# Turning the quantized probabilities of the second layer by transposing DMAs

## The chip, the core and the metric

The kernel runs on one core of a Trainium2 chip. The core has a matrix engine (TensorE, PE in the profile, its weight loads PEld), a vector engine (VectorE, DVE), an activation engine (ScalarE, ACT), a general engine (GpSimd, POOL) and a queue engine (SyncE, SP) that issues DMAs. Matmuls and transposes on TensorE write to PSUM, from where VectorE or ScalarE has to copy the result to SBUF. DMAs move data between SBUF and device memory, or inside SBUF, on 16 DMA engines that all queues share. The metric is the device time of one execution in microseconds; less is better.

## The reference

Four transformer layers are applied in a row to `x` (16 sequences of 128 tokens, width 256, 16 heads of 16 features). The change concerns the second layer, whose two attentions work with numbers rounded to 8 bits:

```python
def _fq(x, delta, zp, n_bits):
    xi = _round_ste(x / delta) + zp
    xq = jnp.clip(xi, 0.0, 2.0 ** n_bits - 1.0)
    return (xq - zp) * delta

def _attn(x, ctx, wq, wk, wv, wo, bo, dq, dk, dv, dw):
    ...
    sim = jnp.einsum('bhid,bhjd->bhij', _fq(q, dq, 128.0, 8), _fq(k, dk, 128.0, 8)) * SCALE
    attn = jax.nn.softmax(sim, axis=-1)
    out = jnp.einsum('bhij,bhjd->bhid', _fq(attn, dw, 0.0, 8), _fq(v, dv, 128.0, 8))
    out = out.transpose(0, 2, 1, 3).reshape(b, n, D)
    return out @ wo + bo

h1 = _ln(x, ln1_g, ln1_b)
x = _attn(h1, h1, a1_wq, ...) + x
h2 = _ln(x, ln2_g, ln2_b)
x = _attn(h2, context, a2_wq, ...) + x
```

The probabilities `attn`, divided by the step `dw`, rounded and clipped, are whole numbers from 0 to 255, which bf16 holds exactly. The first, third and fourth layers use unrounded attentions and feed-forward blocks in float32.

## The kernel before

**Tiling.** The 16 sequences are split into 8 groups of two (`GB = 2`). `group(g)` (line 1330) writes down all steps of one group through the four layers; all eight groups can be under way together (`LIVE = 8`). Most working tiles are blocks cut out of one SBUF arena (kind `m`, called `arena` in the profile). PSUM has four slots of 2 KB per partition (`pw`) and a single one of 8 KB (`ps`) for attention scores.

**The stage of the change.** `quantized_attention` (line 1045) runs twice per group (`i = 0, 1`). It makes rounded queries, keys and values and calls `attention` (line 886), its only caller. For each of the two sequences `j`, `begin` computes the scores of all 16 heads into `ps`; then for each half `c` of eight heads `soft` (line 1097) makes the row maximum (line 1099), subtracts it (1112), takes the exponential (1118), sums and inverts (1124 to 1127), scales and rounds on GpSimd (eight instructions at line 1133) and clips into a bf16 block `eb` of 128 queries x 8 heads x 128 keys (DVE, line 1137). The product with the values needs the keys on the partitions, so `eb` has to be turned: eight 128x128 transposes on TensorE (line 905) into one `pw` slot, and one copy of 128x1024 bf16 to the block `eT`, on ScalarE (line 910) or VectorE (line 911). When both halves are there, `products` (line 867, sixteen matmuls at line 879) multiplies them with the values, and line 1143 scales the result. There are 8 groups x 2 attentions x 2 sequences x 2 halves = 64 such turns, and 32 products. The `dtype == F32` side of `attention` is not used here; the float32 attentions have a function of their own, whose products also appear at line 879.

**The order.** Nothing is scheduled on the chip: `Plan.order()` (line 217) writes the instruction order of every engine out in advance. Each step lists its possible engines with a price in us; the loop takes the step that can start earliest, ties being broken by its depth plus an entry of the table `LEADS` for its group and stage. A DMA step on SP is taken to be there at its price plus `LOAD = 2.2` plus an own extra after it starts (line 414). Blocks with a role are limited per stage by the counts given to `plan.enter` (line 889). On the chip every engine runs its list strictly in order, so an instruction that waits holds back all that stand behind it on that engine. All DMAs go through SP: weights (`weight`, line 629, 256 KB each, at most three in a stage), the first layer's rearrangements through device memory (lines 952, 974, 1029, 1036), and kept keys and values (lines 1192, 1216). SP too waits in order, for the data to store or for the place to load into.

Of the kernel before, what the change touches and what calls it, by code (L numbers as in the profile page):

```python
# [8 lines left out]
F32 = mybir.dt.float32  # L9
# [7 lines left out]
P = 128  # L17
B, S, D, H, DH, FF = 16, 128, 256, 16, 16, 1024
# [54 lines left out]


LEADS = [
    [83, 27, 167, 130, 306, 193, 74, 226, 213, -45, 163, -53, 159, -84, 116, -64, 214, 400, 286, 283],
    [-69, -856, -114, -260, -60, 57, -165, -14, -2, -22, -386, -90, 144, -71, -260, -59, -586, -159, -213, -106],
    [49, -47, -11, 314, -162, 407, 51, 168, -361, -27, -172, 141, -4, -107, 36, 5, -54, 235, 78, 92],
    [-16, -228, 250, -173, -19, 106, 36, 203, -176, 14, 164, 2, 299, -144, 10, 309, -45, 154, 150, -1],
    [210, 166, 422, 222, 201, 790, 324, 499, 569, 334, 435, 116, 502, 205, 259, 760, 536, 716, 652, 178],  # L80
    [330, 158, 210, 147, 392, 517, 262, 488, 490, 57, 292, 77, 380, 208, 348, 38, 542, 447, 523, 1141],
    [267, 148, 130, 158, 333, 376, 220, 605, 204, -29, 43, 216, 340, 164, 196, 435, 324, 999, 754, 951],
    [288, 156, 593, 320, 407, 313, 255, 389, 233, 323, -30, 86, 440, 164, 213, 583, 372, 760, 452, 550],
]
CONTEXT = 18
HANDOVER = {"PE": 0.25, "-": 0.0}
# [65 lines left out]
class Plan:  # L152
# [3 lines left out]
    def block(self, kind, shape, dtype=F32, role=None):  # L156
        b = Block(kind, shape, dtype)
        if role is not None:
            sec = self.section
            b.section, b.role, b.turn = sec, role, sec.made[role]  # L160
            sec.made[role] += 1
            sec.units[role] = max(sec.units[role], b.units)
        return b
# [264 lines left out]
def decoder_stack_kernel(ctx: ExitStack, tc: tile.TileContext, a: dict, out: bass.AP):  # L428
    nc = tc.nc
    V, A, G, T = nc.vector, nc.scalar, nc.gpsimd, nc.tensor  # L430
# [7 lines left out]
    ident = const.tile([P, P], F32, tag="ident", name="ident")  # L438
    make_identity(nc, ident)
    ident_b = const.tile([P, P], BF16, tag="identb", name="ident_b")  # L440
# [70 lines left out]
    plan = Plan()  # L511
    step, block = plan.step, plan.block
# [4 lines left out]
    def psum(dtype=F32, shape=(P, 2, NT)):  # L517
        return block("pw", shape, dtype)
# [110 lines left out]
    def weight(source):  # L629

        t = block("m", [P, 2, D], role="w")
        t.source = source.tensor.name, source.offset
        step(
            [("SP", 1.3, lambda: nc.sync.dma_start(out=t.ap(), in_=source.rearrange("(k p) m -> p k m", p=P)))],
            writes=[t],
        )
        return t
# [44 lines left out]
    def tokens_first(w, t, ps, lhs=None, start=True, stop=True, reads=(), holds=()):  # L682


        def issue():
            for j in range(GB):
                for k in range(2):
                    T.matmul(  # L688
                        ps.ap()[:, j, :], lhsT=lhs(k, j) if lhs else t.ap()[:, k, j * S : (j + 1) * S],
                        rhs=w.ap()[:, k, :], start=start and j + k == 0, stop=stop and j == GB - 1 and k == 1,  # L690
                    )

        step([("PE", 1.72, issue)], reads=[w, *([t] if t else []), *reads], writes=[ps], holds=holds)
# [192 lines left out]
    def attention(x, wo, begin, soft, out_of, vz, dtype, after):  # L886


        plan.enter(after=after, w=1, oT=1, e=2, eT=2, **({"r": 1} if dtype == F32 else {"eb": 1}))
        wo = weight(wo)  # L890
        oT = block("m", [P, 2, NT], role="oT")
        for j in range(GB):
            ps, held = begin(j)
            eTs = []
            for c in range(2):
                e = soft(ps, j, c, held[c])
                eT = block("m", [P, 8, S], dtype, role="eT")
                eTs.append(eT)
                per = 4 if dtype == F32 else 8
                for q0 in range(0, 8, per):  # L900
                    pt = block("pw", [P, per, S], dtype)

                    def turn(pt=pt, e=e, q0=q0):
                        for q in range(per):
                            T.transpose(pt.ap()[:, q, :], e.ap()[:, q0 + q, :], ident if dtype == F32 else ident_b)  # L905

                    step([("PE", 0.5, turn)], reads=[e], writes=[pt], holds=[eT])
                    step(
                        [
                            ("ACT", 0.6 if dtype == F32 else 1.2, lambda pt=pt, eT=eT, q0=q0: A.copy(eT.ap()[:, q0 : q0 + per, :], pt.ap())),  # L910
                            ("DVE", 0.66 if dtype == F32 else 0.7, lambda pt=pt, eT=eT, q0=q0: V.tensor_copy(eT.ap()[:, q0 : q0 + per, :], pt.ap())),
                        ],
                        reads=[pt], writes=[(eT, q0)],
                    )
            out_of(oT, eTs, vz, j)
        ps = psum()
        tokens_first(wo, oT, ps)
        add_to(x, ps)
# [551 lines left out]
```

## Time and profile before

| What | us |
|---|---|
| Time, median of 3 runs | 1461.99 (1459.98 to 1463.36) |
| The profiled execution | 1458.82 |
| Its span, first to last instruction | 1456.7 |
| TensorE busy | 1398.3 (96%) |
| VectorE busy | 1010.9 (69%) |
| ScalarE busy | 849.7 (58%) |
| GpSimd busy | 633.3 (43%) |
| DMA queue of SP, share of the 16 engines | 24.5% |

The groups of instructions in the profile are read as: line, engine and operation, output <- input with shape, count, then the busy time of the group and the mean duration of one. TensorE overlaps successive matmuls, so a group's count times its mean is more than the time that it holds the engine; the timeline of starts is the better measure.

### The profile page before, as it was taken

What the parts mean: (1) busy time and instruction counts of PE and PEld (TensorE: products, weight loads), DVE (VectorE), ACT (ScalarE), POOL (GpSimd) and SP (SyncE); (2) the same over time, 40 slices, a digit from 0 to 9 for tenths busy, and PEclk for the clock granted to TensorE, in tenths of its full rate; (3) what the DMA queues carried; (4) which work ended last, traced back from release to release, by engine and by line L of the source; (5) the groups of instructions that cost most, each with busy time, mean ns of one, the idle gap of its engine ahead of it and who ended that gap; (6) DMA issues with size and microseconds to landing.
All of it is one profiled execution on the core that took longest, in us unless ns stands there. A gap on an engine that the chain in (4) does not pass through costs nothing. (4 is left out here: it accounts for less than half of the span.)

```text
span 1456.7 us, 35756 instructions
## 1 busy us (share of the span) xinstructions
PE 1398.3 (96%) x14771; PEld 1141.3 (78%) x14771; DVE 1010.9 (69%) x1555; ACT 849.7 (58%) x1490; POOL 633.3 (43%) x1415
## 2 busy tenths in 40 slices
PE   8899998999899999899999999999999999999998
PEld 6677887878678888687878777777878888787777
DVE  1665788898988779767764976779478766556431
ACT  4565676766776656565554665657556454445552
POOL 2232857455777446524432542545634234243210
PEclk9999998999999999999999999999999999999999
DMA  6566513412432122112211532211210111100000
GB/s 207 138 171 192 188 48 102 117 34 67 125 90 95 44 67 70 56 52 66 84 38 45 160 101 97 85 55 56 73 45 2 42 38 66 31 31 2 2 9 23
DMA packets 138386, 109.67 MB, mean 75 GB/s; under 512 B 72288, under 2 KB 127472, under 8 KB 138096
## 3 DMA queue, kind: packets, MB, share of 16 engines
q1 hardware_dynamic: 138224, 107.40, 24.5%
q8 instruction: 116, 1.90, 0.5%
q14 instruction: 46, 0.38, 0.1%
HBM read 80.11 MB, written 27.26 MB: 74 GB/s over the span
## 5 line engine op out<-in xcount | busy, mean ns | idle before, releaser
L688 PE MATMUL pw<-arena 128*128 128x256 f32 x2048 | 484.2, 387 | 7.3 <-ACT arena L654 3.1
L675 PE MATMUL pw<-arena 128*128 128x256 f32 x2048 | 480.9, 385 | 7.8 <-ACT arena L663 2.5
L688 PEld LDWEIGHTS pw<-arena 128*128 128x128 f32 x2048 | 383.0, 192 | 68.8 <-issue 9.3
L675 PEld LDWEIGHTS pw<-arena 128*128 128x128 f32 x2048 | 379.2, 191 | 71.0 <-issue 10.0
L1133 POOL TENSOR_SCALAR arena<-arena,sm 128x128 f32<-128x128 f32 x512 | 195.9, 403 | 107.7 <-DVE sm L1127 73.4
L1314 DVE RECIPROCAL arena<-pw 128x256 f32<-128x256 f32 x64 | 112.1, 1752 | 104.0 <-PE pw L879 86.8
L734 POOL TENSOR_TENSOR arena<-arena,rows 128x512 f32<-128x512 f32 x107 | 137.7, 1289 | 89.7 <-ACT arena L721 74.0
L833 PE MATMUL ps<-arena 32*128 32x128 f32 (+2 forms) x3328 | 153.0, 309 | 2.8 <-DVE arena L1112 1.1
L1236 DVE TENSOR_REDUCE sm<-ps 128x16 f32<-128x2048 f32 x48 | 109.6, 2283 | 36.3 <-PE ps L833 33.8
L833 PEld LDWEIGHTS ps<-arena 32*128 32x128 f32 x3072 | 116.1, 186 | 20.4 <-issue 12.0
L696 DVE TENSOR_TENSOR arena<-pw,arena 128x512 f32<-128x512 f32 x88 | 60.3, 685 | 101.2 <-PE pw L688 99.7
L801 ACT ACTIVATE arena<-pw,cols_sb 128x256 f32<-128x256 f32 x184 | 78.0, 472 | 68.3 <-PE pw L675 65.5
L1261 POOL CAST mq<-sm 128x16 bf16<-128x16 f32 x58 | 15.8, 273 | 234.2 <-DVE sm L1236 114.6
L710 POOL TENSOR_SCALAR sm<-sm 128x2 f32<-128x2 f32 x88 | 20.6, 234 | 215.0 <-DVE sm L705 200.1
L721 ACT ACTIVATE arena<-arena,sm,sm 128x256 f32<-128x256 f32 x149 | 83.2, 597 | 49.3 <-POOL sm L714 48.7
L663 ACT ACTIVATE arena<-pw,cols_sb 128x256 f32<-128x256 f32 x140 | 72.7, 563 | 50.5 <-PE pw L647 47.0
L1275 ACT COPY arena<-pw 128x512 bf16<-128x512 bf16 x64 | 37.3, 582 | 84.5 <-PE pw L1271 77.6
L879 PE MATMUL pw<-arena 128*32 128x128 f32 (+1 forms) x2560 | 82.9, 265 | 3.4 <-ACT arena L910 3.0
L1099 DVE TENSOR_REDUCE sm<-ps 128x8 f32<-128x1024 f32 x64 | 77.6, 1213 | 9.8 <-PE ps L833 9.5
L1302 ACT ACTIVATE arena<-ps 128x1024 f32<-128x1024 f32 x64 | 64.1, 1025 | 33.1 <-PE ps L833 30.3
L647 PE MATMUL pw<-ident,arena 128*128 128x128 f32 x416 | 66.8, 286 | 15.1 <-DMA arena<-in_x_dram 5.1
L910 ACT COPY arena<-pw 128x1024 bf16<-128x1024 bf16 x56 | 56.3, 1011 | 41.9 <-PE pw L905 37.2
(142 smaller groups left out, 1993.8 us busy)
## 6 DMA issues: line engine op xcount, KB each, us to landing
arena<-in_L_xattn_ff_w_dram SPq DMA_DIRECT2D x38, 256.0 KB, 3.0
mha<-arena SPq DMA_DIRECT2D x16, 512.0 KB, 4.5
ca<-arena SPq DMA_DIRECT2D x16, 512.0 KB, 3.9
arena<-mha SPq DMA_DIRECT2D x16, 512.0 KB, 4.4
arena<-ca SPq DMA_DIRECT2D x16, 512.0 KB, 4.5
dqkv<-arena SPq DMA_DIRECT2D x8, 768.0 KB, 4.0
arena<-dqkv SPq DMA_DIRECT2D x16, 384.0 KB, 4.3
arena<-in_L_xattn_W_dram SPq DMA_DIRECT2D x24, 256.0 KB, 2.8
```

The source lines that it names most:

```text
L663: ("ACT", 0.54, lambda c=c: A.activation(dst.ap()[:, c, :], ps.ap()[:, c, :], AF.Identity, bias=biases(c), scale=scales(c))),
L675: T.matmul(ps.ap()[:, m, :], lhsT=w.ap()[:, k, m * P : (m + 1) * P], rhs=t.ap()[:, k, :], start=(k == 0), stop=(k == 1),)
L688: T.matmul(ps.ap()[:, j, :], lhsT=lhs(k, j) if lhs else t.ap()[:, k, j * S : (j + 1) * S], rhs=w.ap()[:, k, :], start=start and j + k == 0 ...
L721: ("ACT", 0.6, lambda j=j: A.activation(xh.ap()[:, j, :], x.ap()[:, j, :], AF.Identity, bias=nb.ap()[:, j : j + 1], scale=rstd.ap()[:, j : ...
L734: ("POOL", 1.33, lambda: G.tensor_tensor(dst.ap(), src.ap(), row(name), op)),
L801: "ACT", 0.47, lambda ps=ps, h=h, m=m, bias=bias: A.activation(h.ap()[:, m, :], ps.ap()[:, m, :], func, bias=bias),
L833: T.matmul(ps.ap()[:, s, c] if i is None else ps.ap()[:, s, c, i], lhsT=left(r, c) if i is None else left(r, c, i), rhs=right(r, c), start ...
L879: T.matmul(po.ap()[32 * s : 32 * s + 32, 2 * ones + c, :], lhsT=lhsT, rhs=eTs[c].ap()[:, 2 * s + i, :], start=(i == 0), stop=(i == 1),)
L1099: step([("DVE", 1.22, lambda: V.tensor_reduce(paired(m.ap()), ps.ap()[:, :, c], AX.X, ALU.max, negate=True))], reads=[ps], writes=[m])
L1133: G.tensor_scalar(e.ap()[:, q, :], e.ap()[:, q, :], r.ap()[:, q : q + 1], MAGIC, ALU.mult, ALU.add)
L1236: V.tensor_reduce(m.ap(), ps.ap().rearrange("p s c i k -> p (s c i) k"), AX.X, ALU.max, negate=True)
L1314: step([("DVE", 1.75, lambda po=po, r=r: V.reciprocal(r.ap(), po.ap()[:, 2:4, :]))], reads=[po], writes=[r])
```

## The change

The eight transposes and the copy of each turn are replaced by one DMA issued by SP that transposes in flight, from `eb` in SBUF to `eT` in SBUF (256 KB, bf16). Its price in the plan is 1.2 with an extra of 1.0, so that the plan takes its result to be there 1.2 + 2.2 + 1.0 = 4.4 us after it starts. The stage may hold two `eb` blocks in place of one, and the table `LEADS` has other numbers, so the instruction order of every engine differs throughout the kernel. The turn no longer uses a `pw` slot.

```diff
 LEADS = [
-    [83, 27, 167, 130, 306, 193, 74, 226, 213, -45, 163, -53, 159, -84, 116, -64, 214, 400, 286, 283],
...
+    [17, -123, 275, 177, 313, 413, 69, 330, 469, -222, 295, 20, 190, -607, -60, 168, 130, 288, 268, -9],
...
 ]
...
     def attention(x, wo, begin, soft, out_of, vz, dtype, after):
-        plan.enter(after=after, w=1, oT=1, e=2, eT=2, **({"r": 1} if dtype == F32 else {"eb": 1}))
+        plan.enter(after=after, w=1, oT=1, e=2, eT=2, **({"r": 1} if dtype == F32 else {"eb": 2}))
...
                 e = soft(ps, j, c, held[c])
                 eT = block("m", [P, 8, S], dtype, role="eT")
                 eTs.append(eT)
-                per = 4 if dtype == F32 else 8
-                for q0 in range(0, 8, per):
-                    pt = block("pw", [P, per, S], dtype)
-
-                    def turn(pt=pt, e=e, q0=q0):
-                        for q in range(per):
-                            T.transpose(pt.ap()[:, q, :], e.ap()[:, q0 + q, :], ident if dtype == F32 else ident_b)
-
-                    step([("PE", 0.5, turn)], reads=[e], writes=[pt], holds=[eT])
-                    step(
-                        [
-                            ("ACT", 0.6 if dtype == F32 else 1.2, lambda pt=pt, eT=eT, q0=q0: A.copy(eT.ap()[:, q0 : q0 + per, :], pt.ap())),
-                            ("DVE", 0.66 if dtype == F32 else 0.7, lambda pt=pt, eT=eT, q0=q0: V.tensor_copy(eT.ap()[:, q0 : q0 + per, :], pt.ap())),
-                        ],
-                        reads=[pt], writes=[(eT, q0)],
-                    )
+                step(
+                    [("SP", 1.2, lambda e=e, eT=eT: nc.sync.dma_start_transpose(out=eT.ap(), in_=e.ap().rearrange("p q k -> p (q k)")), None, 1.0)],
+                    reads=[e], writes=[eT],
+                )
             out_of(oT, eTs, vz, j)
```

## The prediction

> **What bounds the kernel now.** I read the page's busy shares first, then its chain of waits, then the group of the removed instructions, and last the DMA issues that resemble the added one.
>
> ```profile
> PE 1398.3 (96%) x14771; PEld 1141.3 (78%) x14771; DVE 1010.9 (69%) x1555; ACT 849.7 (58%) x1490; POOL 633.3 (43%) x1415
> ...
> PE 29%; DVE 1%; ACT 0%; issue 0%; ACTq 0%
> ```
>
> TensorE is busy for 1398.3 of 1456.7 us, so it idles for only 58.4. The chain that ended last, which the profile follows back over the last 30% of the span, is matmul after matmul. So TensorE's own list of work is the bound, and time taken off it is worth close to its length as long as nothing makes TensorE wait instead. Time taken off ScalarE (58% busy) is worth nothing by itself.
>
> The next fence is the groups by line; the two lines after the dots are the answer for line 905 by stages of the span (us, then TensorE and weight-load busy time of that line alone).
>
> ```profile
> L905 PE MATMUL pw<-ident_b,arena 128*128 128x128 bf16 x512 | 40.2, 222 | 5.2 <-DVE arena L1137 2.6 <-DVE arena L1315 1.1 <-ACT arena L1058 0.9
> L905 PEld LDWEIGHTS <-arena 128*128 128x128 bf16 x512 | 32.2, 99 | 16.3 <-DVE arena L1137 7.0 <-issue 5.0 <-DVE arena L696 0.3
> L910 ACT COPY arena<-pw 128x1024 bf16<-128x1024 bf16 x56 | 56.3, 1011 | 41.9 <-PE pw L905 37.2 <-issue 3.5 <-ACT arena L1058 0.7
> ...
> 150.00:400.00 250.00, 14.99 (x184) 12.08 (x184) 0.97 0.32 96
> ...
> sum 1457.00, PE 40.17 PEld 32.22; mean PE 6.69 PEld 5.37
> ```
>
> The 512 transposes have a busy time of 40.2 us, but that counts the overlap with their neighbours. The timeline of TensorE shows what they really hold it for:
>
> ```profile
> 817.00 1.89 PE L688 MATMUL pw<-arena 128*128 128x256 f32 x8
> 818.73 0.61 PE L905 MATMUL pw<-ident_b,arena 128*128 128x128 bf16 x8
> 819.17 3.67 PE L675 MATMUL pw<-arena 128*128 128x256 f32 x16
> 822.68 0.61 PE L905 MATMUL pw<-ident_b,arena 128*128 128x128 bf16 x8
> 823.13 1.95 PE L688 MATMUL pw<-arena 128*128 128x256 f32 x8
> ```
>
> The start of the transposes lies 0.44 and 0.45 us ahead of the start of the next matmul. Added up over all rows of line 905 in the timeline, with the idle time shown in the next row taken out, it is 33.2 us, or 0.52 per turn.
>
> The added operation does not occur in this trace: no DMA transposes. The nearest are DMAs cut into short pieces, in the answers for lines 974 and 1029 (issue time in ns as min/median/max) and in the list of DMA issues (KB each, median us from issue to landing):
>
> ```profile
> L974 SPq DMA_DIRECT2D arena<-dqkv x16: 359/377/1157, 25.4 to 832.0; - x16
> ...
> DMA to landing us min/median/max: 3.6/4.3/6.3
> ```
>
> ```profile
> L1029 SPq DMA_DIRECT2D do<-arena x64: 313/486/1837, 47.9 to 857.3; - x64
> ```
>
> ```profile
> do<-arena SPq DMA_DIRECT2D x64, 32.0 KB, 2.3
> ...
> arena<-in_L_xattn_W_dram SPq DMA_DIRECT2D x24, 256.0 KB, 2.8
> ```
>
> **The change part by part.** The sum is made against the profiled execution: 1458.82 us, of which 1456.7 are span and 2.1 lie around it. The median of the runs is 3.2 us above it.
>
> *Removed from TensorE:* 64 turns of eight transposes, 33.2 us by the timeline; the 40.2 us of the group is the upper bound. The 5.2 us that TensorE idled ahead of them (the bf16 block was late, or the slot) is not counted as gained, because what stands behind may wait in its place. So -33.
>
> *Removed from ScalarE and VectorE:* 56 copies of 1011 ns, 56.3 us, and 8 of 680 ns, 5.4 us. Both engines work beside TensorE, so this is 0. What it could bring is less waiting of TensorE for these engines. For the products, the answer for line 879 puts only 3.0 us down to line 910 and 0.8 to line 911, so 0 to -4; I take 0. If ScalarE were no longer covered by TensorE, the 56.3 us would be the price, on the gaining side.
>
> *A `pw` slot freed 64 times, one more `eb` block (2 KB per partition), new numbers in `LEADS`:* these move the order of everything. The bounds are the 58.4 us of TensorE idle time, of which an order could regain a part, and on the other side a little more idle than now. The idle per stage, from busy times by windows, is 18.5 us before 150 us, 13.6 up to 400, 7.2 up to 700, 7.2 up to 1000, 3.7 up to 1110 and 8.5 after. Without transposes in it, the first and the last stretch can only change by reordering. I take 0 and keep 15 us, a quarter of the idle time, for either side.
>
> *Added: 64 transposing DMAs on SP.* SP issues for 364.6 us of the span (its timeline rows added up), 252 of them between 150 and 1110 us, where the turns lie: 26% of that stretch. Each new DMA carries 256 KB. The lower bound is a weight load of the same bytes: about 0.37 us of issue and 2.8 to landing. The nearest row in kind is the load from `dqkv`, whose 384 KB come in runs of 192 bytes (48 floats), much like rows of 128 bf16: 0.377 us of issue, 4.3 to landing. The upper bound is the finest cut row, `do`, with runs of 64 bytes: 32 KB per DMA at a mean issue of 0.56 us (36.1 us for the rows of line 1029, over 64). Eight of those make 256 KB: 8 x 0.56 = 4.4 us of SP, and 2.3 + 7 x 0.56 = 6.2 to landing. Below nothing it can't go, since a DMA only adds to SP. I take the `dqkv` row: it is nearest in bytes and in run length.
>
> What that means for TensorE depends on when the order expects the result. The order puts the product 4.4 us or more after the DMA's start. At 4.3 us to landing, TensorE does not wait for it. What is queued behind the DMA on SP are weight loads and the first layer's stores and loads; they now also wait until `eb` is written by line 1137 on VectorE, and those who wait for them are matmuls at lines 675 and 688. The chain from the scores to `eb` is planned ahead, but VectorE or GpSimd late by some tenths of a microsecond now holds SP, where before it held TensorE itself (7.0 + 2.6 us at lines 905 in all). I put 6 us for products and loads that come late: about 0.1 us for each of the 64 turns, or two thirds of the 9.6 us that the old turns made TensorE wait. The bounds are 0 and the case worked out as the second rival. The DMA engines are at 22% to 32% in these stretches by the windows; 64 x 256 KB are 16.8 MB against 107.4 on that queue now, so at the same cost per byte 24.5% becomes 28%, which is no bound.
>
> *Sum:* -33 + 0 + 0 + 6 = -27; 1458.8 - 27 = 1431.8 for a profiled execution, and 3 more for the median of the runs: **1435 us**.
>
> [...] The timeline has eight transposes holding TensorE for 0.45 us, 56 ns each, because they are pipelined. [...]
>
> **The rivals.** *First: the gain is there but turns into idle time.* Profile for it: every turn now passes through SP, which already waits in order for TensorE and VectorE (119.5 us in 23 waits of weight loads for line 688 alone), and one late weight load costs all of TensorE. Against it: 96% busy leaves little room for such waits, and there are mostly several groups' matmuls to choose from. With 33 us of new idle, the time is 1459 to 1465, say 1462: no change.
>
> *Second, on the other side: the DMA is slower than the order believes.* At the upper bound, 6.2 us to landing, the second half's result is 1.8 us behind the 4.4 of the order; 32 products on TensorE wait for it: 58 us. SP is held for 4.4 us where the order has 1.2, 64 x 3.2 = 205 us; charged at SP's present share of 26%, the part that meets another DMA about to go, that delays loads that TensorE waits for by 53 us. 1462 - 33 + 58 + 53 = 1540 us. It decides from 33 / 32 = 1.0 us of lateness per product, that is from about 5.4 us to landing. For it: no row shows a DMA that rearranges two-byte elements, and the `dqkv` loads alone already reach 6.3 us at most. Against it: those loads have a median of 4.3 and an issue of 0.377 us. [...]
>
> *Third: more than the sum.* The freed slot and ScalarE let the order close a quarter of the idle time, 15 us: 1420. For it: 37.2 us in which ScalarE waited at line 910 for the transposes are gone, and four `pw` slots serve all groups. Against it: the waits of TensorE that name ScalarE or VectorE are a few us per line.
>
> **How the numbers follow.** The forecast case, 1422 to 1452, gets 0.52; more than the sum 0.06; no net gain 0.08, half of it within 0.2% of the present time and the rest split evenly on both sides; slower by the second mechanism up to 1550 gets 0.22, and beyond 1550 0.12. 0.2% (3 us) is about what a measurement of this kernel can tell from no change. Faster: 0.52 + 0.06 + 0.02 = 0.60; same 0.04; slower 0.02 + 0.22 + 0.12 = 0.36. The range from 1416 to 1550 leaves out some 0.03 below and 0.12 above; the forecast's own range is 1422 to 1452.
>
> **What would show it.** In the changed kernel's profile: lines 905, 910 and 911 are gone; TensorE's busy time is about 1360; the list of DMA issues has 64 transposing DMAs with their time to landing, near 4.3 us if I am right and above 5.4 if the second rival is; TensorE's waits at line 879 that name a DMA add up to less than 10 us if I am right and to some 60 if the rival is; the SP rows show whether the issue is nearer 0.4 or 4 us. The prediction would be wrong if SP is held for long by each transposing DMA, if weight loads land later in the stretches from 150 to 1110 us, or if the new order leaves TensorE idle before 150 or after 1110 us, where nothing was removed.

## The result and the profile after

The change moved the time by nothing that can be measured: 1462.11 us in the median of 12 runs (1459.87 to 1466.35), beside 1461.92 us for the kernel before (12 runs, 1458.57 to 1463.78). The ratio is 1.0005, with a 95% interval from 0.9993 to 1.0016. The prediction was 1435 us. 1462 us was the time of its first rival, with a chance of 0.08.

The page of the changed kernel (profiled span 1458.2 us, before 1456.7): busy times, the DMA queue, and the engines in the chain that ended last.

```profile
PE 1377.7 (94%) x14259; PEld 1119.9 (77%) x14259; DVE 995.7 (68%) x1522; ACT 803.9 (55%) x1433; POOL 636.0 (44%) x1413
...
q1 hardware_dynamic: 206896, 125.23, 31.8%
...
PE 81%; DVE 9%; ACT 3%; POOL 2%; issue 1%; DMA 0%; SPq 0%; ACTq 0%; DVEq 0%; POOLq 0%
```

The 512 transposes are gone from the count of matmuls (14771 to 14259), ScalarE lost 46 us, and still the span is as long. TensorE's busy time fell by 20.6 us only, though 33.2 us of work had left it. The chain now reaches back over nearly the whole span (before, over the last 30%), and DVE, ACT and POOL hold 14% of the span in it.

The new operation itself, the answer for its line (issue times in ns as min/median/max; below it, who waited for it, in us and times):

```profile
L900 SPq DMA_TRANSPOSE arena<-arena x64: 1231/1239/2121, 180.6 to 1042.9; - x64
...
who waited for it (us, times):
  PE pw L879: 1.2, 2
...
DMA to landing us min/median/max: 3.0/3.1/5.7
```

It lands 3.1 us after its issue, sooner than the 4.4 us that the order allows. It holds SP for 1.24 us, as the plan's price of 1.2 says. The products wait for it for 1.2 us in all.

Where the time went is seen by stages. Columns: window, us, busy time (and instructions) of PE, PEld, DVE, ACT and POOL, granted TensorE clock, DMA share, GB/s. First before, then after:

```profile
150.00:400.00 250.00, 236.38 (x2179) 194.64 (x2172) 214.18 (x374) 173.76 (x331) 156.82 (x337) 0.97 0.32 96
400.00:700.00 300.00, 292.77 (x2900) 238.74 (x2899) 236.80 (x341) 184.79 (x300) 159.33 (x357) 0.99 0.22 68
700.00:1000.00 300.00, 292.80 (x3556) 237.04 (x3555) 218.65 (x318) 174.86 (x289) 126.88 (x288) 1.00 0.27 81
```

```profile
150.00:400.00 250.00, 223.82 (x1803) 181.91 (x1802) 215.60 (x360) 157.02 (x295) 159.24 (x339) 0.97 0.48 117
400.00:700.00 300.00, 272.37 (x2779) 219.38 (x2779) 248.92 (x380) 170.39 (x293) 163.56 (x365) 0.95 0.38 99
700.00:1000.00 300.00, 298.73 (x3169) 244.30 (x3168) 202.56 (x287) 168.82 (x278) 131.79 (x305) 1.00 0.26 76
```

Between 150 and 700 us TensorE is not busy for 26.2 + 27.6 = 53.8 us after, and was not for 13.6 + 7.2 = 20.8 us before: 33.0 us more. The turns that lay in this stretch, 44 of the 64, had held it for 23.1 us by the timeline, and outside of it TensorE idles 10.9 us less than before, since work moved as well. So all that was freed here, and more, turned into waiting. The worst place is 490 to 580 us, again before, then after:

```profile
490.00:580.00 90.00, 90.00 (x1107) 73.78 (x1109) 74.50 (x99) 57.30 (x92) 50.23 (x114) 1.00 0.18 56
```

```profile
490.00:580.00 90.00, 65.15 (x765) 49.78 (x765) 84.52 (x125) 51.85 (x101) 54.47 (x128) 0.85 0.54 138
```

TensorE, full before, is idle for 25 us of 90 there, and the clock that it is granted falls from 1.00 to 0.85. Its timeline in this place (start, length, instruction, and in brackets the idle time ahead and what ended it):

```profile
497.91 0.61 PE L844 MATMUL ps<-arena,three 32*128 32x512 bf16 x4 [2.33 <-DVE arena L1234]
...
502.71 0.40 PE L833 MATMUL ps<-arena 32*128 32x256 bf16 x8 [1.65 <-DVE arena L1283]
...
510.83 0.61 PE L844 MATMUL ps<-arena,three 32*128 32x512 bf16 x4 [3.80 <-ACT arena L1093]
...
517.31 0.40 PE L833 MATMUL ps<-arena 32*128 32x256 bf16 x8 [1.38 <-DVE arena L1283]
```

All four wait for the single `ps` slot: the step that reads the last scores out of it, on VectorE or ScalarE, isn't done. Over the whole span this is where most of the new waiting is: ahead of the scores (lines 833 and 844) TensorE idles 23.7 us in all, before the change 6.0. Their larger group, before and then after (the last column is the idle time ahead of it):

```profile
L833 PE MATMUL ps<-arena 32*128 32x128 f32 (+2 forms) x3328 | 153.0, 309 | 2.8 <-DVE arena L1112 1.1
```

```profile
L833 PE MATMUL ps<-arena 32*128 32x128 f32 (+2 forms) x3328 | 155.4, 313 | 13.4 <-DVE arena L1100 6.9
```

What filled the stretch from 490 to 580 us before are the large matmuls of the linear layers, at lines 688 and 675. The groups of the same stretch, before and then after (busy us, mean ns of one | idle before them):

```profile
L688 PE MATMUL pw<-arena 128*128 128x256 f32 x128 | 30.3, 384 | 0.0
L675 PE MATMUL pw<-arena 128*128 128x256 f32 x119 | 28.0, 384 | 0.0
```

```profile
L688 PE MATMUL pw<-arena 128*128 128x256 f32 x85 | 26.1, 460 | 2.5 <-ACT arena L654 2.4
...
L675 PE MATMUL pw<-arena 128*128 128x256 f32 x40 | 10.4, 405 | 0.9 <-DMA arena<-in_L_xattn_mha_wk_dram 0.8 <-DMA arena<-in_L_xattn_ca_kw_dram 0.2
```

The old order has 247 of them here, the new one 125, and each takes longer (460 and 405 ns in place of 384) at the lower clock (0.85 in place of 1.00).

Added up over TensorE's whole timeline, the idle time in brackets is 53.7 us before and 76.1 us after, 22.4 more. The mean granted clock is 0.993 before and 0.982 after. If matmuls slow down as the clock does, that is (1/0.982 - 1/0.993) x 1380 = 15.6 us at TensorE's some 1380 us of work. The balance is -33.2 + 22.4 + 15.6 = +4.8 us; the spans differ by +1.5. The clock term is an estimate from these means. Read off the busy time it is smaller: that fell by 20.6 us where 33.2 us of work had left, so the matmuls that stayed kept TensorE busy for 12.6 us longer, and -33.2 + 12.6 + 22.1 (22.1 us being what it is longer not busy, 80.5 after and 58.4 before) is +1.5. Not all of that need be the clock: the groups by line and shape add up to 7.7 us more than before, the two largest, lines 688 and 675, to 2.5 of these; the rest, 4.9, is overlap of successive matmuls that is missing.

### The profile page after: what moved, and what is told of

Read it like the earlier page. It is cut to its first block, busy times and chain, and to the rows that moved or that the text cites. A ratio compares the mean times of both kernels' runs of the same rounds, so it can differ in the third digit from the quotient of the medians.

```text
span 1458.2 us, 34691 instructions
## 1 busy us (share of the span) xinstructions
PE 1377.7 (94%) x14259; PEld 1119.9 (77%) x14259; DVE 995.7 (68%) x1522; ACT 803.9 (55%) x1433; POOL 636.0 (44%) x1413
## 3 DMA queue, kind: packets, MB, share of 16 engines
q1 hardware_dynamic: 206896, 125.23, 31.8%
## 4 chain that ended last, share of the span: by engine, by line
PE 81%; DVE 9%; ACT 3%; POOL 2%; issue 1%; DMA 0%; SPq 0%; ACTq 0%; DVEq 0%; POOLq 0%
PE pw L675 28%; PE pw L688 27%; PE ps L833 9%; PE pw L879 8%; PE ps L844 4%; PE pw L647 2%; DVE sm L1087 1%; PE pw L1259 1%; POOL arena L1121 1%; DVE arena L1100 1%; DVE sm L1112 1%; DVE arena L1283 1%; PE pw L1007 1%; DVE arena L1125 1%; PE pw L974 1%
## 5 line engine op out<-in xcount | busy, mean ns | idle before, releaser
L1121 POOL TENSOR_SCALAR arena<-arena,sm 128x128 f32<-128x128 f32 x512 | 198.9, 413 | 103.7 <-DVE sm L1115 74.1
L734 POOL TENSOR_TENSOR arena<-arena,rows 128x512 f32<-128x512 f32 x105 | 134.5, 1282 | 96.2 <-ACT arena L721 79.0
L833 PEld LDWEIGHTS ps<-arena 32*128 32x128 f32 x3072 | 118.5, 190 | 21.9 <-issue 12.0
L1290 ACT ACTIVATE arena<-ps 128x1024 f32<-128x1024 f32 x64 | 64.4, 1024 | 54.7 <-PE ps L833 41.5
L1106 ACT ACTIVATE arena<-arena,sc 128x1024 f32<-128x1024 f32 x63 | 72.0, 1147 | 30.9 <-DVE arena L1100 30.7
```

What stands on the lines that cost most here:

```text
L734: ("POOL", 1.33, lambda: G.tensor_tensor(dst.ap(), src.ap(), row(name), op)),
L833: T.matmul(ps.ap()[:, s, c] if i is None else ps.ap()[:, s, c, i], lhsT=left(r, c) if i is None else left(r, c, i), rhs=right(r, c), start ...
L1121: G.tensor_scalar(e.ap()[:, q, :], e.ap()[:, q, :], r.ap()[:, q : q + 1], MAGIC, ALU.mult, ALU.add)
```

## The experiments

Two questions: did the transposing DMA cost something, and is TensorE's time worth its length at all in this stage? **Theory A** is the prediction's: TensorE is the bound, so the 33 us are there, and something new ate them. **Theory B**: between 150 and 1010 us TensorE's list, run in order, is cut by waits for the other engines, and time taken off it turns mostly into longer waits. The further letters in the expectations split these, and are explained where they first stand in the text below. Each kernel is compared with the kernel before on the same chip, whose median was 1460.1 to 1460.5 us. Lines behind 886 are 12 lower in kernels made from the changed one.

### TensorE's work removed, and doubled, in the old order

Only the first of the eight transposes of each turn is issued; the copy repeats it. Order, slots and queues stay.

```diff
-                        for q in range(per):
-                            T.transpose(pt.ap()[:, q, :], e.ap()[:, q0 + q, :], ident if dtype == F32 else ident_b)
+                        T.transpose(pt.ap()[:, 0, :], e.ap()[:, q0, :], ident_b)
...
-                            ("ACT", 0.6 if dtype == F32 else 1.2, lambda pt=pt, eT=eT, q0=q0: A.copy(eT.ap()[:, q0 : q0 + per, :], pt.ap())),
+                            ("ACT", 0.6 if dtype == F32 else 1.2, lambda pt=pt, eT=eT, q0=q0: A.copy(eT.ap()[:, q0 : q0 + per, :], pt.ap()[:, 0:1, :].to_broadcast([P, per, S]))),
```

> The kernel before, its order of every engine kept line by line; of the eight TensorE transposes of each turn only the first is issued, and the copy from PSUM repeats that one head for all eight (so the output is not the reference's: seven of eight heads of the second layer's attentions use the first head's probabilities). It takes the removed TensorE time away without any DMA and without another order. Theory A (TensorE's list is the bound, and the gain of the change was lost in its new written order): 7/8 of 33.2 us, 29 us, minus at most 9 us of new waits: 1433 to 1443 us, ratio 0.980 to 0.987. Theory B (VectorE or the chains between the engines bind together with TensorE, so that TensorE time is not worth its length): 1452 us or more, ratio above 0.993. Theory C (the transposing DMAs disturb) says nothing here and goes with A.

Measured: 1451.74 us, ratio 0.9939 (0.9925 to 0.9954). By the timeline the turns hold TensorE for 8.0 us where it was 33.2, so 25.2 us are gone, and the time fell by 8.3 (the profiled span by 5.4). Idle time rose by 13.3 us, and the clock fell from 0.993 to 0.988, 7.0 us by the same reckoning as above: -25.2 + 13.3 + 7.0 = -4.9. There is no DMA and no new order, and ScalarE's copies take as long as before (1012 ns, where it was 1011). TensorE's time in this stage is worth about a third of its length (0.27 to 0.43 by the interval). A's range is missed by 9 us; the time is 0.3 us below what B gave as its least.

The other direction issues each turn's transposes twice:

```diff
-                        for q in range(per):
+                        for q in (*range(per), *range(per)):
```

> The kernel before, its order kept, each turn's eight transposes issued twice into the same place (output as the reference). It adds 8 x 56 ns x 64 = 29 us to TensorE alone. Theory A (TensorE's list is the bound over the whole span): 1485 to 1495 us. Theory F (between 150 and 1010 us, where 56 of the 64 turns lie, TensorE's list is cut by waits for the other engines that take up what it gains or loses): 1465 to 1475 us, the mirror of the 8 us that leaving out seven of eight transposes gained.

Measured: 1477.75 us, ratio 1.0115 (1.0085 to 1.0145). The turns hold TensorE for 59.9 us, 26.7 more, and the time rose by 17.5: between the two ranges, nearer to F, which holds that part of any change is taken up by the waits. Idle time fell by 4.7 us. Time added costs two thirds of its length (0.46 to 0.79 by the interval), time removed brings one third.

### The DMA by itself

The changed kernel with its order, but a plain DMA of the first eighth of each block in place of the transposing one, and products that read that piece.

```diff
-                            rhs=eTs[c].ap()[:, 2 * s + i, :], start=(i == 0), stop=(i == 1),
+                            rhs=eTs[c].ap()[:, 0 if hasattr(eTs[c], "first_only") else 2 * s + i, :], start=(i == 0), stop=(i == 1),
...
-                    [("SP", 1.2, lambda e=e, eT=eT: nc.sync.dma_start_transpose(out=eT.ap(), in_=e.ap().rearrange("p q k -> p (q k)")), None, 1.0)],
+                    [("SP", 1.2, lambda e=e, eT=eT: nc.sync.dma_start(out=eT.ap()[:, 0, :], in_=e.ap()[:, 0, :]), None, 1.0)],
```

> The changed kernel, its order kept line by line; each transposing DMA of 256 KB is replaced by a plain DMA of its first 32 KB from the clipped block to the turned block, and the products read that one piece for all heads (so the output is not the reference's: nothing is turned, and seven of eight heads' probabilities are left out). Same waits before it, an eighth of the bytes, 0.4 us of SP in place of 1.24. Theory A (the transposing DMA itself costs nothing on the path): within 5 us of the changed kernel, 1457 to 1467 us. Theory C (its landing, its hold on SP or its load on the DMA engines costs the gain): 1445 us or less.

Measured: 1461.05 us, ratio 1.0002 (0.9989 to 1.0015). With an eighth of the bytes and no transposing, the time is the same. In the order that was made for it, the DMA's bytes, its landing and its 1.24 us on SP cost nothing that can be measured. What the run leaves as it was is SP's waiting for the clipped block ahead of each DMA (224.4 us in 39 waits in this run), so it doesn't price what stands behind it.

### The DMA in the old order

The kernel before, with the DMA issued by SP at the place in the order where TensorE turned; the step of the copy stays in its place but issues nothing, and there is one `eb` block as before.

```diff
-                    def turn(pt=pt, e=e, q0=q0):
-                        for q in range(per):
-                            T.transpose(pt.ap()[:, q, :], e.ap()[:, q0 + q, :], ident if dtype == F32 else ident_b)
+                    def turn(e=e, eT=eT):
+                        nc.sync.dma_start_transpose(out=eT.ap(), in_=e.ap().rearrange("p q k -> p (q k)"))
...
-                            ("ACT", 0.6 if dtype == F32 else 1.2, lambda pt=pt, eT=eT, q0=q0: A.copy(eT.ap()[:, q0 : q0 + per, :], pt.ap())),
+                            ("ACT", 0.6 if dtype == F32 else 1.2, lambda: None),
```

> The kernel before with its order kept; each turn's eight transposes are replaced, at their own place in the order, by the transposing DMA, and the copy from PSUM issues nothing. Output as the reference. Theory A: -33 us on TensorE, and in the old order 19 of the 32 products start less than 3.3 us after the last turn; their shortfalls to a landing of 3.1 us add up to some 29 us, and SP, which now waits for VectorE in the old order's places, adds 0 to 20: 1455 to 1480 us, ratio 0.995 to 1.012. Theory C (SP waiting in order for the clipped block holds back weight loads, and that is what costs): 1500 us or more. Theory B: about 33 us above A, 1490 to 1510.

Measured: 1500.06 us, ratio 1.0268 (1.0253 to 1.0283): far above A's range, in B's and at the edge of C's, so it doesn't tell these two apart. The answer for the DMA's line:

```profile
L904 SPq DMA_TRANSPOSE arena<-arena x64: 1231/1232/2202, 149.4 to 1137.1; - x64
...
who waited for it (us, times):
  PE pw L879: 23.1, 13
  DVE arena L1137: 20.4, 8
  ACT arena L663: 12.4, 5
...
```

and SP's own waits ahead of it:

```profile
SPq L904 <- DVE arena L1137: 104.9, 25, 19.5
```

The DMA lands as fast as in the changed kernel (3.1 us), but it starts late: SP stands for 104.9 us in 25 waits for the clipped block, with all its other transfers behind it. The products then wait 23.1 us for the DMA, and the next clip (line 1137) waits 20.4 us for the only `eb` block. ScalarE too waits for the DMA, for 25.6 us over all its lines, most likely because the emptied step of the copy keeps its wait; such waits would come from this edit, not from the DMA. How long SP stands is not what costs by itself, for in the changed kernel it stands longer, and there the products wait 1.2 us:

```profile
SPq L900 <- DVE arena L1125: 183.9, 30, 30.1
```

Nor do late weight loads show on TensorE, as C has it: its waits for other DMAs than these add up to 9.3 us, before the change to 7.9. What the old order lacks is room between the DMA and what needs its result; that is argued, not tried by itself. Would another queue do? The same kernel with the DMA issued by ScalarE:

```diff
-                        nc.sync.dma_start_transpose(out=eT.ap(), in_=e.ap().rearrange("p q k -> p (q k)"))
+                        nc.scalar.dma_start_transpose(out=eT.ap(), in_=e.ap().rearrange("p q k -> p (q k)"))
```

> The kernel before, its order kept, with each turn made by the transposing DMA at the turn's place, as in the run with 1500 us, but issued by ScalarE in place of SP (the copy from PSUM issues nothing, so ScalarE's list keeps its length; output as the reference). Theory H (in the old order the 40 us were lost on SP: weight loads behind a DMA that waits for the clipped block): those loads go out in time again and what stays is the landing 2 us later than the copy, 1465 to 1480 us. Theory I (the later landing alone lost them): 1495 us or more.

Measured: 1525.87 us, ratio 1.0452 (1.0426 to 1.0479). H, by which SP's queue was the trouble, missed by 46 us. The time lies in I's range, but I's reason, the later landing alone, isn't shown by it: ScalarE's list is run in order too (in the kernel before it stood at line 910 for 37.2 us in 20 waits for the transposes), and what stands behind the clip here are activations. Line 1137 waits 27.0 us for the DMA and the products 21.9, much as with SP.

### The order by itself

The changed code with the `LEADS` of the kernel before.

```diff
-    [17, -123, 275, 177, 313, 413, 69, 330, 469, -222, 295, 20, 190, -607, -60, 168, 130, 288, 268, -9],
+    [83, 27, 167, 130, 306, 193, 74, 226, 213, -45, 163, -53, 159, -84, 116, -64, 214, 400, 286, 283],
...
```

> The changed kernel with the table LEADS of the kernel before, nothing else. The kernel's own planner gives the written orders these lengths: before 1442.0 us, changed kernel 1443.3, this one 1536.9. Theory A (the written order decides, and the planner's length foretells it; the change had lost its gain on paper already): 1556 us, within 12. Theories B and C have no reason for a change of this size from the table alone; if the chip's waits for DMAs or VectorE are what binds, 1462 to 1500.

Measured: 1549.83 us, ratio 1.0611 (1.0596 to 1.0627). The same instructions as in the changed kernel, sorted by other numbers, take 88 us more (144.6 us idle, clock 0.961). The table is a larger term than the whole change. The plan's own length foretells it: 1536.9 us here, 1443.3 for the changed kernel, 1442.0 for the kernel before. So, as far as the plan tells, the gain was missing from the written order already.

### Is VectorE what TensorE waits for?

VectorE is busy for 84.5 of the 90 us in the worst stretch. Theory D makes that the cause, E the written order itself. To tell, the maximum and the sum of the quantized softmax are taken over 16 of 128 keys, which takes some 111 us off VectorE. In both kernels:

```diff
-            step([("DVE", 1.22, lambda: V.tensor_reduce(paired(m.ap()), ps.ap()[:, :, c], AX.X, ALU.max, negate=True))], reads=[ps], writes=[m])
+            step([("DVE", 1.22, lambda: V.tensor_reduce(paired(m.ap()), ps.ap()[:, :, c, :, : S // 8], AX.X, ALU.max, negate=True))], reads=[ps], writes=[m])
...
-                    V.tensor_reduce(r.ap(), e.ap(), AX.X, ALU.add)
+                    V.tensor_reduce(r.ap(), e.ap()[:, :, : S // 8], AX.X, ALU.add)
```

> The kernel before, its order kept line by line, with two VectorE instructions of each half of eight heads made short: the row maximum and the row sum of the quantized attentions look at 16 of the 128 keys (so maxima, sums and with them the output are not the reference's). That takes about 64 x 1.0 + 61 x 1.0 = 125 us from VectorE and nothing from TensorE. Theory D (TensorE and VectorE bind in turns, stretch by stretch, and time taken from one alone comes back mostly as its idle time): TensorE keeps its 1398 us, so at most some of its 54 to 58 us of idle time goes: 1435 to 1455 us. Theory E (TensorE's freed time in the changed kernel was lost to something else, such as ScalarE's chains or SP): the same here, 1435 to 1455.

> The changed kernel, its order kept line by line, with the same two VectorE instructions made short, about 125 us of VectorE in all (output not the reference's, as in the run beside it). Theory D: with VectorE out of the way in the stretch from 490 to 580 us, the freed TensorE time shows: 15 to 40 us below the same edit of the kernel before, 1405 to 1430 us. Theory E: within 8 us of the same edit of the kernel before.

Measured: 1446.58 us from the kernel before (ratio 0.9911, 0.9892 to 0.993), and 1448.82 us from the changed one (0.9924, 0.9901 to 0.9947). The stretch of the changed kernel, with the lighter VectorE:

```profile
490.00:580.00 90.00, 69.93 (x868) 54.05 (x869) 74.64 (x139) 57.00 (x113) 58.92 (x139) 0.85 0.59 146
```

VectorE has room now (74.6 of 90), and TensorE still idles 20 us there, at the same clock. D is refuted for the changed kernel; both kernels gain alike, 111 us of VectorE being worth 12 to 14. Then both removals at once, one transpose per turn and the light VectorE in the old order (the edits are those above):

> The kernel before, its order kept, with both edits that were run alone: only the first transpose of each turn (-8 us when alone) and the row maximum and row sum of the quantized attentions over 16 of 128 keys (-14 us when alone); the output is not the reference's. Theory D (TensorE and VectorE bind in turns, each hiding the other's gain): more than the sum, 1425 us or less. Theory F (each gain is cut by waits of its own): the sum, 1434 to 1442 us.

Measured: 1445.49 us, ratio 0.9892 (0.9868 to 0.9916), only 1 us below the light VectorE alone. D's range is missed by 20 us and F's, the sum of the two gains, by 3, though the interval (1441 to 1448 us) still touches it. The profile, of the fastest execution (1439.40 us), shows 8.7 us more idle time than with the light VectorE alone (56.8 and 48.1), and a clock of 0.990 for 0.996. Why the two don't add up isn't settled.

### Both forms with their order searched anew

If the new order was merely a poor one, a better table should bring out the gain. Both kernels got new numbers for `LEADS` from searches of equal length, judged by the plan's own length; that of the changed kernel started from a table that was already 4.9 us shorter than its own. The kernel before, with nothing else changed:

```python
LEADS = [
    [6071, 4436, 8406, 6262, 9498, -6735, -6214, -4612, 10099, -17722, -880, -17776, 6370, -6264, 11144, -12566, 5129, 26739, 22783, -5362],
    [-5492, -25327, 1229, 1296, -54, -5867, -21503, -10545, -4018, -7273, -27140, -12241, 6175, -9745, -15266, -1139, -9294, -3062, -4987, 9406],
    [4956, 1995, -4, 9528, -17259, 22657, -10438, 5609, -15517, -9176, -7420, 632, -13867, -7528, 986, 4532, 5785, 13622, 6851, -9328],
    [1145, -8523, 9256, -18444, -7718, 5372, -3403, 5342, -5968, -6785, -5625, -5278, 7110, 7440, -6134, 12622, -9952, 8404, 6417, 3115],
    [8828, 6810, 15800, 4272, 7851, 13913, 3262, 17685, 6999, -4905, -1818, 11358, -16980, 10932, -225, 11288, 11176, 13949, 21433, 21446],
    [11357, 7494, 1777, -5215, -4409, 2966, -1068, 14761, -1990, 5691, 62, 5004, 17089, 5145, 2050, -2287, 967, -2009, 14169, -16466],
    [10383, -3067, 3602, -2540, 10925, 14293, -1355, 14411, 16601, -3064, 3302, 8148, 16556, 6074, 3196, 15063, 11941, 19303, 19432, 24148],
    [12950, -2641, 23265, 4928, 9300, -2008, -3015, 10100, 6273, -8576, -14615, -1487, 14840, 7923, 9305, 33765, -357, 16466, 13922, 17214],
]
```

and the changed kernel:

```diff
-    [17, -123, 275, 177, 313, 413, 69, 330, 469, -222, 295, 20, 190, -607, -60, 168, 130, 288, 268, -9],
+    [8088, 116, 4221, 3617, 11100, 6905, 64, 17530, 9977, -18936, -5113, -8862, 29053, -35, 5646, -5072, -1630, 23210, 15582, -13915],
...
```

> The kernel before, with nothing changed but the numbers in LEADS, which come from a long search of the kernel's own plan (the plan's length falls from 1442.0 to 1433.5 us). Theory G (the written order decides, and the plan tells small differences truly): 8.5 us less than the kernel before, 1449 to 1455. Theory J (the plan's length says little at this size, since it knows neither late releases nor the granted clock of TensorE): anything from 1455 to 1475.

> The kernel after, with nothing changed but the numbers in LEADS, from a search of the same length as that of before_retuned (the plan's length falls from 1443.3 to 1430.2 us, 3.3 below before_retuned). Theory G: 11.8 us less than the kernel before, 1446 to 1452, and 0 to 6 us less than before_retuned, so that of the 33 us of TensorE some 3 can be had in the end. Theory J: 1455 to 1475, no relation to before_retuned. If the 33 us were only hidden by a poorly chosen order, it should be 15 us or more below before_retuned.

Measured: the kernel before 1450.36 us (ratio 0.9933, 0.992 to 0.9946), the changed one 1456.31 us (0.9971, 0.996 to 0.9982). For the kernel before G hit, by which the written order decides and the plan tells small differences truly. For the changed kernel it missed by 4 us beyond its range, and the time is one that J allows, by which the plan says little at this size: the plan puts it 3.3 us ahead, and it is 6.0 us behind. This better order does not bring out the gain, and the fastest of the kernels that give the reference's output is the old form with a new table. By windows the pair repeats the first: between 150 and 700 us TensorE is not busy for 20.1 us in the re-tuned old form and for 51.0 in the new one, 30.9 more. The idle time only lies elsewhere, at 250 to 300 us:

```profile
250.00:300.00 50.00, 21.82 (x187) 14.78 (x186) 48.49 (x73) 21.51 (x30) 28.91 (x69) 0.67 0.26 48
```

```profile
276.09 0.62 PE L833 MATMUL ps<-arena 32*128 32x256 bf16 x8 [9.44 <-DVE arena L1100]
...
292.29 0.41 PE L879 MATMUL pw<-arena 128*32 128x128 bf16 x8 [5.87 <-DMA arena<-arena]
```

VectorE is full there (48.5 of 50), and the scores wait 9.44 us for the subtraction at line 1100 to leave `ps`. In this order the DMA isn't free either; over the span the products wait for it:

```profile
PE pw L879 <- DMA arena<-arena: 10.2, 4, 5.9
```

Whether these 10.2 us make the 6.0 us by which the new form is behind, no run shows. The same lightening of VectorE as above, in this kernel:

> after_retuned with the quantized maximum and sum taken over 16 of the 128 keys, as in light_before and light_after (some 110 us less of VectorE, the written order kept; the output is wrong, since seven eighths of the keys are left out of maximum and sum). In after_retuned the stretch from 250 to 300 us has VectorE busy for 48.5 of 50 us and TensorE for 21.8, with waits of TensorE for the softmax's subtraction at line 1100. Theory K (in this order VectorE's softmax work is what TensorE waits for): the stretch closes, TensorE idles 25 us less there, its granted clock rises with it, and the time falls by 25 us or more, to 1431 or less. Theory E (the waits come with the written order, whatever VectorE's load): 11 to 14 us less, as in the pair before, 1442 to 1446.

Measured: 1444.47 us, ratio 0.9894 (0.9874 to 0.9914), in E's range; K is refuted. The stretch and the same wait:

```profile
250.00:300.00 50.00, 27.71 (x208) 19.64 (x206) 34.47 (x79) 21.96 (x34) 37.08 (x87) 0.73 0.37 74
```

```profile
268.18 0.61 PE L833 MATMUL ps<-arena 32*128 32x256 bf16 x8 [10.15 <-DVE arena L1100]
```

With VectorE at 34.5 of 50 us TensorE's longest wait is still 10.15 us, and it still ends at line 1100. VectorE now waits itself, for ScalarE's exponentials (line 1106, 6.4 us) and GpSimd's scaling (1121, 3.7 us). The softmax goes through four engines, each in its written order, and in neither tuned order did relieving VectorE alone close the gap. Whether relieving two of them would, or a second `ps` slot, wasn't tried.

### The balance over all runs

Work is what was taken off TensorE by its timeline, idle the change in the bracketed idle times, clock (1/granted - 1/0.993) x 1380, sum the three together; all against the profile of the kernel before, in us. The column "busy" is a second reading of the clock term, from measured times: the change of TensorE's busy time less the work. It holds slower matmuls and lost overlap together, and isn't in the sum.

| Kernel | work | idle | granted clock | clock | busy | sum | span measured |
|---|---|---|---|---|---|---|---|
| doubled turns | +26.7 | -4.7 | 0.995 | -2.8 | -3.0 | +19.2 | +18.0 |
| light VectorE, before | 0 | -5.6 | 0.996 | -4.2 | -5.4 | -9.8 | -10.5 |
| one transpose, light | -25.2 | +3.1 | 0.990 | +4.2 | +2.9 | -17.9 | -19.2 |
| one transpose | -25.2 | +13.3 | 0.988 | +7.0 | +6.8 | -4.9 | -5.4 |
| light VectorE, after | -33.2 | +13.0 | 0.983 | +14.1 | +11.5 | -6.1 | -9.1 |
| after | -33.2 | +22.4 | 0.982 | +15.6 | +12.6 | +4.8 | +1.5 |
| DMA in old order, SP | -33.2 | +51.7 | 0.975 | +25.7 | +24.9 | +44.2 | +41.3 |
| DMA in old order, ScalarE | -33.2 | +64.4 | 0.968 | +35.9 | +32.4 | +67.1 | +63.3 |
| after, old table | -33.2 | +90.9 | 0.961 | +46.3 | +33.6 | +104.0 | +91.1 |
| before, re-tuned | 0 | -6.2 | 0.990 | +4.2 | -1.4 | -2.0 | -8.1 |
| after, re-tuned | -33.2 | +22.1 | 0.980 | +18.4 | +9.4 | +7.3 | -1.9 |
| after, re-tuned, light | -33.2 | +12.0 | 0.983 | +14.1 | +6.1 | -7.1 | -15.6 |

The first eight agree within 4 us. With the old table and the re-tuned ones the sum is 6 to 13 us too high. The clock term is the roughest, as the mean clock also counts time in which TensorE had nothing to do; one kernel's mean also differs between its executions, 0.989 to 0.994 for the kernel before. In these four rows the busy time gives 6 to 13 us less than the clock, which is most of the misfit, and in "after, re-tuned" the sum even has the wrong sign. By the measured columns most or all of what TensorE's list loses comes back as idle time and as longer busy time of the matmuls that stayed: 20 of 25.2 us with one transpose, 17 of 25.2 with one transpose beside the lighter VectorE, and all of the 33.2 in the changed kernel, with its own table or the re-tuned one, each beside the old form of its kind.

## Why the prediction was wrong

**The step that failed** is the first: "TensorE's own list of work is the bound, and time taken off it is worth close to its length". The chain of waits that I rested it on covered the last 30% of the span, from about 1012 us on. Of the 64 turns 56 lie between 150 and 1012 us, where that chain says nothing. The other support, 96% busy, says that TensorE had little idle time, not that the other engines could deliver faster once it had less to do. One transpose in place of eight measured it: 25.2 us off TensorE brought 8.3. By the same third, the 33.2 us of the change would have brought 11; it brought nothing. That remainder is lost in the new order, since the DMA's bytes, landing and hold cost nothing in it, but no run takes it apart further.

**Point by point.**
- *Removed from TensorE, -33.* The work did go, 512 matmuls of it. TensorE's busy time was to be about 1360; it is 1377.7, because the other matmuls kept TensorE busy for 12.6 us longer, in part at a lower clock (0.982 in place of 0.993 over the span).
- *Freed slot, second `eb` block, new table: 0, with 15 us to either side.* This is the term that was mis-sized: 22.4 us of idle time (with 6.3 us for DMAs, below) and 12.6 us by which the other matmuls kept TensorE busy for longer. I had allowed "a little more idle than now" and had no term for the clock. The fence of line 905 in the prediction showed 0.97 in its own window.
- *Added DMA.* Landing was taken as 4.3 us from the `dqkv` row; it is 3.1. Issue was taken as 0.377 us; it is 1.24, inside the bounds but three times the row. The products wait 1.2 us for it, below the 10 us given.
- *The 6 us for late products and loads.* This term came out near its size: TensorE's waits that end with a DMA are 14.2 us after and 7.9 before, 1.2 of the difference for products and 5.1 for loads (3.9 of it for the context, at 225 and 530 us). Its yardstick was wrong, though: of the 9.6 us, 7.0 are idle time of the weight loads, and only 2.6 that of TensorE's matmuls. The run with an eighth of the DMA leaves SP's waiting in place and still has 12.0 us of such waits.
- *SP's 364.6 us of issue.* The timeline's rows that were added up merge several DMAs with the waits between them; the single issues in the trace add up to 183 us, 117 of them between 150 and 1110 us. The share of 26% in the second rival should have been 12%.
- *DMA share 24.5% to 28%.* It is 31.8%: 17.8 MB more cost 7.3 points of share, where the old bytes cost 24.5 / 107.4 x 17.8 = 4.1. So a transposed byte took about 1.8 times the time of the average one; with the plain DMA of an eighth the share is 25.2% at 110.55 MB, the old rate.
- *Removed from ScalarE, 56 us at 0.* No run tried this alone; it stays open.
- *What would make it wrong.* I had named idle time before 150 or after 1110 us. TensorE is busy for some 2 us more there in both stretches (134.0 and 340.5). The loss lies between 150 and 700 us, where two thirds of the gain were booked (44 of 64 turns).

**The rivals.** The first gave the right time by the right words, gain into idle time, but mostly for the wrong reason: late loads through SP were to cause it, and of the 22.4 us more idle time only 6.3 end with a DMA; the larger part are waits for VectorE and ScalarE, most of them over the `ps` slot. That it named 1462 us to the microsecond is luck. Its counter-argument, that "96% busy leaves little room for such waits", is the failed step once more. The second rival's own condition, 5.4 us to landing, was not met: the median is 3.1, the longest 5.7. Late products do show where the order isn't made for the DMA (23.1 us at 1500 us), but there too the DMA lands in 3.1 us: it starts late. These 3.1 us are no more than a weight load of the same bytes took in the changed kernel (medians of 3.0 and 3.5). In issue (1.24 us, where the 52 loads of the largest group of weights, line 634, had a median of 0.44) and in time per byte (about 1.8 times the average one, by the shares above) it is dearer than these.

## What to carry to other kernels

Ask what an engine's time is worth in the stage where the change is, not over the span: a chain of waits that starts behind that stage is no evidence for it, and a stage like the one from 150 to 700 us here, where VectorE was busy for 82% before the change and ScalarE for 65%, and the work of a group passes through them and back, can turn freed time into waiting. The cheapest test is to leave out part of the work in the unchanged order. Where the order is written out by a search, compare two forms only with both searched alike: here the table alone was worth from -10 to +88 us, the change of form between 0 and +6.

## What the hardware showed that was not expected

Over the 12 kernels of the table and the one before, the granted TensorE clock goes down as the idle time goes up, from 0.996 at 48 us of idle time to 0.961 at 145, close to in order. By the column "busy" the matmuls keep TensorE busy for 39.0 us longer between these ends (-5.4 to +33.6), at the lower clock and with less overlap: 0.4 us for each of the 96.5 us of waiting; in the five runs with over 20 us more idle time than before it is 0.4 to 0.6. It shows where single waits are 3.80 us and less; from 500 to 520 us in the changed kernel:

```profile
500.00:520.00 20.00, 12.46 (x176) 9.73 (x172) 18.45 (x30) 10.89 (x26) 9.62 (x21) 0.71 0.35 93
```

The longest single wait there is 3.80 us, the others 0.23 to 1.65, and the granted clock is 0.71. A stretch with shorter waits only follows close by, from 525 to 540 us:

```profile
525.00:530.00 5.00, 3.22 (x36) 2.06 (x35) 4.93 (x7) 2.83 (x5) 0.89 (x4) 1.00 0.64 149
530.00:535.00 5.00, 2.48 (x8) 1.93 (x9) 4.90 (x6) 2.77 (x3) 2.02 (x6) 0.69 0.55 169
535.00:540.00 5.00, 5.00 (x16) 4.11 (x15) 4.82 (x10) 1.01 (x3) 4.44 (x12) 0.63 0.01 3
```

TensorE's gaps there are 0.83, 0.97 and 2.39 us, all between 528 and 533 us, and the clock is 0.69 and then 0.63. So in this trace three gaps of 2.39 us and less, close together, went with a lower clock as well. No run changed the gaps alone.

The transposing DMA of 256 KB from SBUF to SBUF took 1.24 us of its queue and 3.1 us to landing in the changed kernel and in three other orders (1.25 and 3.2 by ScalarE's queue), against 0.52 us of TensorE and 1.01 us of ScalarE for the turn that it replaces.
